# Layer 2's scores and values in narrow groups of the TensorE array, and its softmax sums taken by ScalarE

## The chip, the cores and the metric

The kernel runs on one core of a Trainium2 chip. The metric is the device time of one execution in microseconds, as the median of three runs. Everything is float32 except two small masks, and an f32 matmul leaves two records in the trace, each of them one pass over the columns of the moving operand.

## The reference

Four cross-attention layers run one after the other on `x` of shape (4, 1024, 256) with a context of shape (4, 77, 256); there are 16 heads. Layer 0 is causal self-attention together with the context, followed by a feed-forward block; layer 1 is a linear attention plus a windowed attention; layers 2 and 3 attend to the 77 context positions only. The change is in layer 2, whose heads are 16 wide:

```python
q = (queries @ Wq.T + bq)...; k = (keys @ Wk.T + bk)...; v = (values @ Wv.T + bv)...   # b h t 16
scores = einsum('bhqd,bhkd->bhqk', q, k) / sqrt(16)
scores = scores * attention_weights                      # (4, 16, 1024, 77), an input
scores = where(attention_mask, -inf, scores)             # an input too
out = einsum('bhqk,bhkd->bhqd', softmax(scores), v)...   # back to b t 256
x = queries + out @ Wo.T + bo                            # then a layer norm, then layer 3
```

## The kernel before

**Layers 0 and 1** take the first three quarters of the time. Each works through batches and quads of heads (`step`): bursts of matmuls for maxima or for weights and sums, and between the bursts pieces of other work, which `jobs0` and `jobs1` list as `Job` objects. A `Job` has a generator, a count of pieces, a stretch of the step in which the pieces are due, and for some a cost in microseconds by which pieces are fitted in. Layer 2's values and keys are made here, long before they are used: `values2` and `keys2` are jobs of batch 0, quad 0. Both write to DRAM (`kept_v`, `kept_k`) through the staging tile `stg` and others that `place` hands out in turn. All DMAs are issued by SyncE (SP) in program order; the next unit's `qk` tiles are filled by DMAs of the same queue (`new_unit`, L792, and `spread`, L377).

The values lie in `kept_v` on a block diagonal: for each half of the heads (8 of them, 616 rows of head and position) every row is 128 wide and holds its 16 values in its head's columns, with zeros elsewhere, which a first DMA writes from a zeroed `stg` (L970).

**Layers 2 and 3** run after that in one loop over slots, `slot23(i)`. There are 32 tiles of 128 queries (4 batches of 8). In slot `i` layer 2 does five stages, each of another tile:

- tile `i` (`a`): `score2` computes the scores of 16 heads x 77 positions = 1232 columns (`HK`), multiplies them with the input weights on VectorE (DVE; L1545), and puts a large negative number where the mask is set (L1550); `maxima2` takes each head's maximum (L1554, L1558);
- tile `i-1` (`p1`): `exps2` runs sixteen exponentials on ScalarE (ACT), one for each head with that head's maximum as bias (L1563); `sums_of` reduces them to the 16 sums on DVE (L1567) and takes the reciprocals (L1570); `divided` multiplies on GpSimd (POOL; L1574);
- tile `i-3` (`p3`): `turned_into` transposes the weights on TensorE (PE) in ten chunks of 128 columns, with three copies out of PSUM by ACT (`pT`, L1376);
- tile `i-4` (`p4`): `values_of2` multiplies the turned weights with `V`, 11 full-width matmuls (chunk 4 serves both halves of the heads) into `pvT`, and ACT copies the result to `oT` (L1593);
- tile `i-5` (`p5`): `out2` projects with `Wo`, `add2` adds to `x` (L1602 on DVE, L1603 on POOL).

Layer 3 follows 12 slots later (`LAG`) with stages of its own: `score3` (PE, then DVE L1626 and L1627), `exp3` (one exponential of 1232 columns, ACT L1643), `sums_of` and `divided`, `turned_into`, and `out3` (20 records into `po`, DVE L1639). So slots 0 to 11 hold layer 2 alone, slots 12 to 36 both layers, and the rest layer 3 alone. Between the stages `more()` runs pieces of side work: `prep2`, the next batch's query projections, and `between`, the norms between the layers. The engines work their queues in program order, and the order in `slot23` is written out by hand.

Score tiles (`pair_tile`) are two PSUM banks each, and there are two of them, shared by both layers. Smaller PSUM tiles (`psT`, `pvT`, projections) share a pool of three, and `po2` and `po3` share one bank. `score2` fills one score tile for each half of the heads, with two matmuls of 64 rows, each against a `kb` whose rows are zero outside the head in question (four heads, 308 columns):

```python
for o in range(2):
    ps = pair_tile()
    for e in range(2):
        r = half_rows(e)
        mm(ps[:, e, 0 : 4 * S].rearrange("p (h s) -> p h s", s=S),
           qT[r, o, P * t : P * t + P], kb[r, o, :, b, :])
```

`loads2(b)` loads a batch's `V` from `kept_v` with five DMAs, and clears part of it on POOL first (L1416); `load_sides` loads each tile's weights and mask.

Of the kernel before, what the change touches and what calls it, by code (L numbers as in the profile page):

```python
# [17 lines left out]
P = 128  # L18
# [13 lines left out]
def tile_xattn_seq(ctx: ExitStack, tc: tile.TileContext, d: dict, out: bass.AP):  # L32
# [899 lines left out]
    kept_g = dram.tile([P, 2, 8, 2, NS], F32, name="kept_g")  # L932
    kept_u = dram.tile([NB, H, S, D], F32, name="kept_u")

    HALF, DIAG = HH * S * P, S * P + DH
    kept_v = dram.tile([NB, 2, HH * DIAG], F32, name="kept_v")
    stg = wpool.tile([P, 1024], F32, name="stg", tag="s7")
    turn = [0]

# [25 lines left out]

    def values2():

        n = NB * 2 * HH * DIAG // P // 8
        nc.gpsimd.memset(stg[:, 0:n], 0.0)
        nc.sync.dma_start(  # L970
            out=kept_v.rearrange("b e x -> (b e x)").rearrange("(p k n) -> p k n", p=P, n=n),
            in_=stg[:, 0:n].unsqueeze(1).to_broadcast([P, 8, n]),
        )
        yield
        for b in range(NB):
            pk = sm.tile([S, D], F32, name="pk", tag="sm")
# [12 lines left out]
    def keys2():  # L989
# [419 lines left out]

    def loads2(b):  # L1410

        V = late.tile([P, NC + 1, P], F32, name="V2", tag="V2", bufs=2)
        lo, hi = [kept_v[b, e, 0:HALF].rearrange("(r n) -> r n", n=P) for e in range(2)]

        k = HH * S % P
        nc.gpsimd.memset(V[:, 4:6, :], 0.0)  # L1416
        nc.sync.dma_start(
            out=V[:, 0:4, :], in_=lo[0 : 4 * P].rearrange("(c p) n -> p c n", p=P)
        )
        nc.sync.dma_start(out=V[0:k, 4, :], in_=lo[4 * P :])  # L1420
        nc.sync.dma_start(out=V[k:P, 5, :], in_=hi[0 : P - k])
        nc.sync.dma_start(
            out=V[:, 6:10, :], in_=hi[P - k : 5 * P - k].rearrange("(c p) n -> p c n", p=P)
        )
        nc.sync.dma_start(out=V[0:HSIZE, 10, :], in_=hi[5 * P - k :])
        shared["v2", b] = V
        yield

# [97 lines left out]
    def score2(a, i):  # L1526

        b, t = a["b"], a["t"]
        qT, kb = shared["b2", b], shared["k2"]
        assert shared["ready2"] >= b  # L1530
        fs, mk = shared.pop(("side", i))
        if i + 1 < NB * NT:
            load_sides(i + 1)
        s = a["s"] = new_scores("s2", 4)
        for o in range(2):
            ps = pair_tile()
            for e in range(2):
# [6 lines left out]
            so = slice(o * HH * S, (o + 1) * HH * S)  # L1544
            nc.vector.tensor_tensor(  # L1545
                s[:, so].rearrange("p (i n) -> p i n", i=2), ps[:, :, 0 : 4 * S],
                fs[:, so].rearrange("p (i n) -> p i n", i=2), ALU.mult,
            )
        sv = s[:, 0:HK]
        nc.vector.copy_predicated(sv, mk, low.to_broadcast([P, HK]))  # L1550
# [7 lines left out]
        nc.vector.tensor_scalar(nm, nm, 0.1 * NEG, -SC, ALU.max, ALU.mult)  # L1558

    def exps2(a, heads):  # L1560
        for h in heads:
            hs = a["s"][:, S * h : S * h + S]
            nc.scalar.activation(hs, hs, AF.Exp, bias=a["nm"][:, h : h + 1], scale=SC)  # L1563

    def sums_of(a, tag):
        den = a["den"] = late.tile([P, H], F32, name=tag, tag=tag)
# [78 lines left out]
    def slot23(i, two, three, more):  # L1645
# [9 lines left out]
        if j < 0:  # L1655
# [13 lines left out]
                add2(p5)  # L1669
            more()  # L1670
            if p1:
                sums_of(p1, "den2")
                divided(p1)
            more()
        elif i < n + 5:
# [35 lines left out]
            more()  # L1711
            if p1:
                divided(p1)
# [36 lines left out]
    def jobs0(b, quad):  # L1750
# [7 lines left out]
        if b == 0 and quad == 0:  # L1758
# [205 lines left out]
```

## Time and profile before

| | |
|---|---|
| median of three runs | 2309.76 us (2304.88 to 2311.91) |
| profiled execution | 2310.56 us, span 2308.8 us, mean granted clock 0.982 |
| PE busy | 2158.3 us, 93% of the span |
| PEld (weight loads) | 1358.9 us, 59% |
| DVE busy | 1506.8 us, 65% |
| ACT busy | 1027.5 us, 45% |
| POOL busy | 652.2 us, 28% |
| DMA | 93.98 MB, mean 41 GB/s |

Busy shares are averages over stages that differ. Layers 2 and 3 take about the last 590 us; their first tile's mask lands at 1725 us, and layer 3's first scores stand at 1828 us. In a group's line the columns are line, engine, operation, names written and read, shape and count, then busy time, the mean of one in ns, and the engine's idle time before them with what ended it. Records of consecutive instructions overlap (a record runs until its own result is out), so for a run of matmuls the time from its first start to the next run's first start is what it takes.

### The profile page before, as it was taken

Reading aid. Unit: us, or ns where it says so; the run is one execution under the profiler, and the core shown is the slowest. Engines: PE = TensorE matmul, PEld = TensorE weight load, DVE = VectorE, ACT = ScalarE, POOL = GpSimd, SP = SyncE. Lnnn points to the kernel's source line nnn. Section 1 sums busy time; section 2 is a strip of 40 time slices with the busy share of each in tenths; the row PEclk is TensorE's granted clock in tenths of the full one; section 3 lists DMA queues with packets and bytes.
Section 4 is the critical chain, followed back from the end, with each engine's and each line's share of the span. In section 5 each row is a group of like instructions: output and inputs, shape, how many; then the busy total and the mean of one; then the engine's idle time right before and its main releaser. Section 6 shows DMA issues by size and latency. Waiting matters only on the chain.

```text
span 2308.8 us, 41140 instructions
## 1 busy us (share of the span) xinstructions
PE 2158.3 (93%) x16842; PEld 1358.9 (59%) x16874; DVE 1506.8 (65%) x2476; ACT 1027.5 (45%) x1716; POOL 652.2 (28%) x959
## 2 busy tenths in 40 slices
PE   4999999999999999999989999999988899999999
PEld 2544444555555455554556665666656678788877
DVE  3756567755566455754375666777748888788654
ACT  1144444434444444344533444544547655555322
POOL 2011113111131112310152233333333444444432
PEclk9899999999999999999989999999999999999999
DMA  7221121100000000101000010111025412313000
GB/s 217 55 57 68 31 65 41 40 6 15 7 15 2 10 11 6 38 1 19 6 15 6 15 26 16 21 20 20 15 74 152 136 51 68 100 49 95 10 10 17
DMA packets 87858, 93.98 MB, mean 41 GB/s; under 512 B 35714, under 2 KB 77558, under 8 KB 87542
## 3 DMA queue, kind: packets, MB, share of 16 engines
q1 hardware_dynamic: 87670, 91.35, 15.2%
q8 instruction: 133, 2.18, 0.4%
q14 instruction: 55, 0.45, 0.1%
HBM read 55.31 MB, written 18.39 MB: 32 GB/s over the span
## 4 chain that ended last, share of the span: by engine, by line
PE 67%; DVE 15%; ACT 4%; issue 2%; POOL 2%; DMA 0%; DVEq 0%; ACTq 0%; POOLq 0%; SPq 0%
PE ps L51 26%; PE po L51 12%; PE pv L51 6%; PE pp L51 5%; PE ph L51 4%; DVE mpart L672 3%; PE pvT L51 2%; DVE ms L1138 2%; PE ppv L51 2%; PE psT L1375 2%; PE pvw L51 1%; DVE mrow L1142 1%; PE pm L590 1%; PE pt L607 1%; ACT pe L738 1%
## 5 line engine op out<-in xcount | busy, mean ns | idle before, releaser
L51 PE MATMUL ps<-qk 32*128 32x192 f32 (+9 forms) x6528 | 581.8, 428 | 57.9 <-DVE mpart L672 25.1
L738 ACT ACTIVATE pe<-ps 128x1024 f32<-128x1024 f32 (+2 forms) x384 | 363.3, 952 | 589.5 <-PE ps L51 579.9
L51 PEld LDWEIGHTS ps<-qk 32*128 32x128 f32 (+1 forms) x6528 | 315.8, 185 | 295.6 <-issue 75.3
L672 DVE TENSOR_REDUCE mpart<-ps 128x2 f32<-128x1024 f32 (+4 forms) x384 | 331.0, 885 | 241.6 <-PE ps L51 240.8
L741 POOL TENSOR_SCALAR_AFFINE_SELECT pe<-pe 128x256 f32<-128x256 f32 (+1 forms) x192 | 95.2, 497 | 665.3 <-ACT pe L738 664.3
L1214 ACT ACTIVATE pew<-ps 128x768 f32<-128x768 f32 x128 | 103.4, 812 | 196.4 <-PE ps L51 196.4
L1574 POOL TENSOR_TENSOR s<-s,den 128x1232 f32<-128x1232 f32 x64 | 144.2, 2254 | 130.2 <-DVE den L1570 125.2
L1219 POOL TENSOR_SCALAR_AFFINE_SELECT pew<-pew 128x512 f32<-128x512 f32 x128 | 81.9, 640 | 337.7 <-ACT pew L1214 337.6
L1138 DVE TENSOR_TENSOR ms<-ps,maskw 128x768 f32<-128x768 f32 x128 | 122.1, 954 | 69.6 <-PE ps L51 68.1
L51 PE MATMUL po<-U,pT 128*128 128x256 f32 (+1 forms) x640 | 147.2, 385 | 10.8 <-DVE x L1602 7.6
L51 PE MATMUL pv<-pe,va 128*32 128x512 f32 (+3 forms) x1536 | 157.1, 496 | 0.0
L51 PE MATMUL ph<-yT,w 128*128 128x256 f32 x512 | 143.1, 401 | 2.4 <-DVE va L401 1.0
L51 PEld LDWEIGHTS po<-U,pT 128*128 128x128 f32 (+1 forms) x640 | 120.3, 192 | 35.0 <-ACT pT L1376 19.6
L51 PEld LDWEIGHTS po<-w,hT 128*128 128x128 f32 x800 | 111.8, 193 | 47.7 <-issue 38.9
L51 PE MATMUL ps<-G,xT 128*128 128x308 f32 x512 | 139.2, 422 | 0.0
L51 PE MATMUL po<-w,hT 128*128 128x128 f32 (+1 forms) x800 | 138.1, 317 | 0.9 <-ACT hT L904 0.9
L1563 ACT ACTIVATE s<-s,nm 128x77 f32<-128x77 f32 x512 | 134.8, 358 | 5.9 <-DVE nm L1558 5.9
L1376 ACT COPY pT<-psT 128x512 f32<-128x512 f32 (+1 forms) x192 | 87.7, 522 | 105.8 <-PE psT L1375 105.2
L665 DVE TENSOR_REDUCE mpart<-ps 128x8 f32<-128x1024 f32 x64 | 78.2, 1225 | 82.6 <-PE ps L51 80.0
L51 PEld LDWEIGHTS ph<-yT,w 128*128 128x128 f32 x512 | 88.8, 192 | 64.0 <-issue 50.8
L1142 DVE TENSOR_REDUCE mrow<-ms 128x4 f32<-128x768 f32 x128 | 122.2, 955 | 4.4
L51 PEld LDWEIGHTS ps<-G,xT 128*128 128x128 f32 x512 | 94.3, 190 | 30.1
(202 smaller groups left out, 3297.6 us busy)
## 6 DMA issues: line engine op xcount, KB each, us to landing
side<-in_fside_t SPq DMA_DIRECT2D x32, 616.0 KB
qk<-st SPq DMA_DIRECT2D x256, 64.0 KB
side<-in_mask_t SPq DMA_DIRECT2D x32, 154.0 KB
G<-kept_g SPq DMA_DIRECT2D x4, 1232.0 KB
U<-kept_u SPq DMA_DIRECT2D x4, 1152.0 KB
x<-in_x SPq DMA_DIRECT2D x8, 512.0 KB
out<-x SPq DMA_DIRECT2D x32, 128.0 KB
kept_g<-st SPq DMA_DIRECT2D x22, 154.0 KB
```

The costliest lines, as they stand in the source:

```text
L51: nc.tensor.matmul(o, lhsT, rhs, start=start, stop=stop, **kw)
L665: nc.vector.tensor_reduce(mpart[self.own][:, :, 2 * p : 2 * p + 2, 0].rearrange("p t j -> p j t"), ps.rearrange("p j (t n) -> p j t n", n= ...
L672: nc.vector.tensor_reduce(mpart[bl][:, i, 2 * p : 2 * p + 2, ci], ps[:, :, o : o + w], axis=AX.X, op=ALU.max,)
L738: nc.scalar.activation(pp[:n, :, o:512], ps[:n, :, o:512], AF.Exp, scale=SC)
L741: nc.gpsimd.affine_select(out=own, in_=own, compare_op=ALU.is_ge, fill=0.0, base=0, pattern=[[0, 2], [0, k], [1, P]], channel_multiplier=-1,)
L1138: nc.vector.tensor_tensor(v, ps.rearrange("p j (i n) -> p j i n", i=2)[:, :, :, 0:n], (maskw[:, 1:2] if w else maskw).unsqueeze(1).to_broa ...
L1142: nc.vector.tensor_reduce(mo, v, axis=AX.X, op=ALU.max, negate=True)
L1214: nc.scalar.activation(pp[:, :, :, 0 : P + WIN], ps.rearrange("p j (i n) -> p j i n", i=2)[:, :, :, 0 : P + WIN], AF.Exp, scale=SC,)
L1219: nc.gpsimd.affine_select(out=pf[:, :, 0:P], in_=pf[:, :, 0:P], compare_op=ALU.is_ge, fill=0.0, base=0, pattern=[[0, 4], [1, P]], channel_ ...
L1376: nc.scalar.copy(pT[:, 4 * group : 4 * group + n, :], ps[:, 0:n, :])
L1563: nc.scalar.activation(hs, hs, AF.Exp, bias=a["nm"][:, h : h + 1], scale=SC)
L1574: nc.gpsimd.tensor_tensor(s3, s3, a["den"].unsqueeze(2).to_broadcast([P, H, S]), ALU.mult)
```

## The change

- `values2` writes each head's values once into `kept_w`, 32 columns wide: a pair of heads (154 rows, `PAIR`) shares the 32 columns, each head in its own 16 and zeros in the other's.
- A new job, `spread2`, copies from `kept_w` to `kept_v` within DRAM. `CUTS` lists the 17 pieces into which the chunks of 128 and the pairs of 154 cut each other; each cut is a 128 x 32 block, zero outside its rows. There is one DMA for each cut, for all batches. `spread2` and `keys2` run in batch 0, quad 1.
- `loads2` is one DMA, without the clearing on POOL.
- `score2` uses 32 rows of the array for two heads at a time: eight matmuls of 154 columns, in four row groups that write four banks. Both score tiles are taken first, and a multiplication covers two banks (two groups, both halves).
- `values_of2` runs 17 matmuls of 32 columns; the four pairs of a half stand in four column groups, and the order goes round the groups.
- `exps2` gives each exponential an `accum_out`, which writes that head's sum into `den2`; DVE's reduction is gone from layer 2 and its reciprocal stays.
- In slots with both layers, `out2` and `add2` move ahead of the transposes of `p3`.

```diff
-    HALF, DIAG = HH * S * P, S * P + DH
-    kept_v = dram.tile([NB, 2, HH * DIAG], F32, name="kept_v")
+    PAIR = 2 * S
+    CUTS = [
+        (c, q, max(P * c, PAIR * q), min(P * c + P, PAIR * q + PAIR))
+        for q in range(HH) for c in range(PAIR * q // P, (PAIR * q + PAIR - 1) // P + 1)
+    ]
+    kept_w = dram.tile([NB, HK, HP], F32, name="kept_w")
+    kept_v = dram.tile([NB, P, len(CUTS), HP], F32, name="kept_v")
...
     def values2():
-        n = NB * 2 * HH * DIAG // P // 8
+        n = len(CUTS) * HP
         nc.gpsimd.memset(stg[:, 0:n], 0.0)
         nc.sync.dma_start(
-            out=kept_v.rearrange("b e x -> (b e x)").rearrange("(p k n) -> p k n", p=P, n=n),
-            in_=stg[:, 0:n].unsqueeze(1).to_broadcast([P, 8, n]),
+            out=kept_v.rearrange("b p k n -> p b (k n)"),
+            in_=stg[:, 0:n].unsqueeze(1).to_broadcast([P, NB, n]),
+        )
+        nc.sync.dma_start(
+            out=kept_w.rearrange("b (s q) n -> s b (q n)", s=S),
+            in_=stg[:S, 0 : H * HP].unsqueeze(1).to_broadcast([S, NB, H * HP]),
         )
...
             for e in range(2):
-                to = kept_v[b, e].rearrange("(j x) -> j x", x=DIAG)[:, 0 : S * P]
                 nc.sync.dma_start(
-                    out=to.rearrange("j (s p) -> s j p", p=P)[:, :, 0:DH],
-                    in_=v[:, P * e : P * e + P].rearrange("s (j r) -> s j r", r=DH),
+                    out=kept_w[b].rearrange("(q e s) n -> e s q n", e=2, s=S)[e, :, :, DH * e : DH * e + DH],
+                    in_=v.rearrange("s (q e r) -> s q e r", e=2, r=DH)[:, :, e, :],
                 )
+            yield
+
+    def spread2():
+
+        for k, (c, q, lo, hi) in enumerate(CUTS):
+            nc.sync.dma_start(
+                out=kept_v[:, lo - P * c : hi - P * c, k, :], in_=kept_w[:, lo:hi, :]
+            )
             yield
...
     def loads2(b):
-        V = late.tile([P, NC + 1, P], F32, name="V2", tag="V2", bufs=2)
...
+        V = late.tile([P, len(CUTS), HP], F32, name="V2", tag="V2", bufs=2)
+        nc.sync.dma_start(out=V, in_=kept_v[b])
...
         s = a["s"] = new_scores("s2", 4)
+        pair = [pair_tile() for _ in range(2)]
         for o in range(2):
-            ps = pair_tile()
-            for e in range(2):
-                r = half_rows(e)
+            for g in range(4):
+                e = 2 * (g % 2)
                 mm(
-                    ps[:, e, 0 : 4 * S].rearrange("p (h s) -> p h s", s=S),
-                    qT[r, o, P * t : P * t + P],
-                    kb[r, o, :, b, :],
+                    pair[g // 2][:, g % 2, PAIR * o : PAIR * o + PAIR].rearrange(
+                        "p (h s) -> p h s", s=S
+                    ),
+                    qT[rows_of(g), o, P * t : P * t + P], kb[rows_of(g), o, e : e + 2, b, :],
+                    skip_group_check=True,
                 )
...
+        for k in range(2):
             nc.vector.tensor_tensor(
...
+                of_pair(s, k),
+                pair[k][:, :, 0 : 2 * PAIR].rearrange("p i (o n) -> p i o n", o=2),
+                of_pair(fs, k), ALU.mult,
             )
...
     def exps2(a, heads):
+        if "den" not in a:
+            a["den"] = late.tile([P, H], F32, name="den2", tag="den2")
         for h in heads:
             hs = a["s"][:, S * h : S * h + S]
-            nc.scalar.activation(hs, hs, AF.Exp, bias=a["nm"][:, h : h + 1], scale=SC)
+            nc.scalar.activation(
+                hs, hs, AF.Exp, bias=a["nm"][:, h : h + 1], scale=SC,
+                accum_out=a["den"][:, h : h + 1],
+            )
...
-        for k in range(NC + 1):
-            o, c = (0, k) if k < 5 else (1, k - 1)
-            r = slice(0, rows_in(c))
-            mm(pv[:, o, :], V[r, k, :], a["pT"][r, c, :], start=k in (0, 5), stop=k in (4, NC))
+        for o in range(2):
+            own = [
+                [(k, c) for k, (c, q, _, _) in enumerate(CUTS) if q == 4 * o + j] for j in range(4)
+            ]
+            for n in range(max(map(len, own))):
+                for j in range(4):
+                    if n < len(own[j]):
+                        k, c = own[j][n]
+                        mm(
+                            pv[rows_of(j), o, :], V[:, k, :], a["pT"][:, c, :],
+                            start=(n == 0), stop=(n == len(own[j]) - 1), skip_group_check=True,
+                        )
...
             if p1:
-                sums_of(p1, "den2")
+                nc.vector.reciprocal(p1["den"], p1["den"])
                 divided(p1)
...
+            if p5:
+                out2(p5)
+                add2(p5)
             if p3:
                 turned_into(p3, "pT2")
             if c:
                 exp3(c)
             if p1:
-                sums_of(p1, "den2")
-            if p5:
-                out2(p5)
-                add2(p5)
+                nc.vector.reciprocal(p1["den"], p1["den"])
...
             j.append(Job(values2(), 5, 0.3, 0.9, us=0.85))
+        if (b, quad) == (0, 1):
+            j.append(Job(spread2(), len(CUTS), 0.1, 0.9))
             j.append(Job(keys2(), 4, 0.5, 0.9, us=0.5))
```

More of the change, by code (lines that the diff above doesn't have):

```diff
@@ L1410, in loads2 @@
     def loads2(b):
-        V = late.tile([P, NC + 1, P], F32, name="V2", tag="V2", bufs=2)
[L1413 to L1425, printed above, removed]
+        V = late.tile([P, len(CUTS), HP], F32, name="V2", tag="V2", bufs=2)
+        nc.sync.dma_start(out=V, in_=kept_v[b])
         shared["v2", b] = V
@@ L1534, in score2, with of_pair @@
         s = a["s"] = new_scores("s2", 4)
+        pair = [pair_tile() for _ in range(2)]
         for o in range(2):
-            ps = pair_tile()
-            for e in range(2):
-                r = half_rows(e)
-                mm(
-                    ps[:, e, 0 : 4 * S].rearrange("p (h s) -> p h s", s=S),
-                    qT[r, o, P * t : P * t + P],
-                    kb[r, o, :, b, :],
-                )
-            so = slice(o * HH * S, (o + 1) * HH * S)
+            for g in range(4):
+                e = 2 * (g % 2)
+                mm(
+                    pair[g // 2][:, g % 2, PAIR * o : PAIR * o + PAIR].rearrange(
[3 more added lines that the diff above has]
+                    skip_group_check=True,
+                )
+        def of_pair(v, k):
+            v = v[:, 0:HK].rearrange("p (o g n) -> p g o n", o=2, g=4)
+            return v[:, 2 * k : 2 * k + 2]
+        for k in range(2):
             nc.vector.tensor_tensor(
-                s[:, so].rearrange("p (i n) -> p i n", i=2), ps[:, :, 0 : 4 * S],
-                fs[:, so].rearrange("p (i n) -> p i n", i=2), ALU.mult,
+                of_pair(s, k),
+                pair[k][:, :, 0 : 2 * PAIR].rearrange("p i (o n) -> p i o n", o=2),
+                of_pair(fs, k), ALU.mult,
             )
```

## The prediction

> **What bounds the kernel now.** I read the stretches of layers 2 and 3 first (busy microseconds by engine: PE, PEld, DVE, ACT, POOL, then the granted clock and DMA), because all but a sliver of the change runs there.
>
> ```profile
> 1725.00:1833.00 108.00, 90.78 (x533) 69.22 (x530) 93.58 (x123) 73.76 (x247) 40.19 (x48) 0.91 0.40 120
> 1833.00:2000.00 167.00, 164.41 (x932) 131.62 (x931) 136.58 (x203) 94.08 (x263) 78.44 (x93) 1.00 0.32 95
> 2000.00:2170.00 170.00, 163.79 (x954) 136.83 (x953) 144.23 (x207) 88.65 (x255) 75.21 (x89) 0.99 0.19 57
> ```
>
> There are two regimes. From 1833 to 2170 layers 2 and 3 run together and TensorE is busy 328.20 of 337 us: PE time taken out of a slot comes off the end. From 1725 to 1833 layer 2 runs alone, and no engine is full. The chain of waits, asked for 1780 to 1797, says what paces a plain slot there:
>
> ```profile
> 1781.39 1.61 DVE s L1550
> ...
> 1783.02 1.45 DVE nm L1554
> ...
> 1784.58 0.42 DVE x L1602
> 1784.99 1.35 DVE den L1567
> ...
> 1786.55 1.45 DVE s L1545 x2
> 1787.99 0.02 issue
> 1788.02 1.63 DVE s L1550
> ```
>
> VectorE runs without a gap, 6.63 us a slot (1781.39 to 1788.02). The timeline gives ScalarE's exponentials in that slot and, further on, TensorE's scores and values:
>
> ```profile
> 1784.81 4.11 ACT L1563 ACTIVATE s<-s,nm 128x77 f32<-128x77 f32 x16
> ...
> 1892.00 2.62 PE L51 MATMUL pvT<-pT,V 128*128 128x128 f32 x22
> ...
> 1894.46 4.31 PE L51 MATMUL ps<-G,xT 128*128 128x308 f32 x16
> ...
> 1901.75 1.31 PE L51 MATMUL ps<-kb,qT 64*128 64x308 f32 x8
> ...
> 1902.99 3.29 PE L51 MATMUL po<-U,pT 128*128 128x256 f32 x14
> ```
>
> An f32 matmul leaves two records, each one pass over its columns. Start to next start, the values take 2.46 us (1892.00 to 1894.46) and the scores 1.24 us (1901.75 to 1902.99). What narrow groups side by side cost is shown by layer 0, which uses them already (32 rows by 128 columns for scores, 128 by 32 for values). The timeline of TensorE alone:
>
> ```profile
> 603.47 1.06 PE L51 MATMUL pv<-pe,va 128*32 128x512 f32 x8
> 604.46 1.16 PE L51 MATMUL po<-w,hT 128*128 128x128 f32 x8
> 605.55 0.71 PE L51 MATMUL ps<-qk 32*128 32x256 f32 x8
> 606.20 1.07 PE L51 MATMUL pv<-pe,va 128*32 128x384 f32 x16
> ...
> 611.20 0.64 PE L51 MATMUL pv<-pe,va 128*32 128x256 f32 x8
> 611.77 1.16 PE L51 MATMUL po<-w,hT 128*128 128x128 f32 x8
> ```
>
> Last, the groups by form from 1740 to the end, for the price of an exponential and of the sum:
>
> ```profile
> L1563 ACT ACTIVATE s<-s,nm 128x77 f32<-128x77 f32 x480 | 126.5, 359 | 4.9 <-DVE nm L1558 4.9
> L1567 DVE TENSOR_REDUCE den<-s 128x16 f32<-128x1232 f32 x63 | 89.6, 1422 | 4.1 <-ACT s L1643 3.9 <-issue 0.3
> L1643 ACT ACTIVATE s<-s 128x1232 f32<-128x1232 f32 x32 | 39.7, 1242 | 42.3 <-DVE s L1627 42.3
> ```
>
> **Values.** 11 full matmuls become 17 of 32 columns in five rounds of up to four (the second half's third round has one). Column-group rows: 8 records of 512 columns take 0.99 us, 8 of 256 take 0.57, so 0.205 ns per column and record, and 0.15 us fixed. Five full rounds are 40 x 128 = 5120 columns: 1.05 + 0.15 = 1.20; only the 34 records that exist: 4352 columns, 1.04. Entering a narrow mode from full width costs another 0.09 us by the start-to-start times of such pairs in the trace. I take 1.31 - the dearer count, because the lone cut stands last. Saving: 2.46 - 1.31 = 1.15 us a tile; between 1.33 and, if the groups ran only two by two, about 0.3.
>
> The Trainium skill (TensorEngine Tiling (Array Packing), section Theoretical Speedup) promises up to 4x for 32 columns; that would be 0.61 us, a saving of 1.85 a tile, and 24 tiles of it would put the time about 17 us under my forecast. The rows above are why I don't take it.
>
> **Scores.** Four matmuls of 64 rows and 308 columns become eight of 32 rows and 154 columns: 16 records, 2464 columns. The row-group burst of 8 x 256 = 2048 columns took 0.65 us (605.55 to 606.20); 416 more at 0.205 ns give 0.74. Saving 0.50 us a tile; modes were switched before too. Each multiply (L1545) now waits for both halves of the scores, so the first may start 0.1 us later; behind it on DVE stand the other multiply and the mask. With layer 3 beside it PE is what is full, alone DVE gains slack below, so I cost it at nothing. Both score buffers are taken at once; their last readers, layer 3's subtractions, end while PE runs about 2 us of transposes.
>
> **Sums.** The reduction L1567 goes for layer 2: 32 x 1.42 = 45 us of DVE work. With both layers it lies beside PE and is worth nothing; alone it is 1.35 us of a 6.63 us slot. The reciprocal stays and, as before, waits for the last exponential. In its place each of 512 exponentials also writes a sum. No row shows that. Below: nothing (a gain is excluded, the exponential itself stays). Above: a whole second short ACT instruction; from 359 ns at 77 columns and 1242 at 1232 the slope is 0.765 ns, the fixed part 0.30 us. Sixteen exponentials take 4.11 us, one every 0.256, so 0.10 us of each record overlaps the next. The nearest row is that overlap: if a sum must be out before the next starts, it is lost. I take e = 0.10 us each and keep 0 and 0.30.
>
> The Trainium skill speaks against me here: VectorE: DVE Perf Modes (section Two Vector instructions with no wait between them) counts an accumulator output as two instructions, on VectorE; if ScalarE did so at the fixed 280 ns less 93 ns overlap that ScalarE: Activation LUTs (What ACT_TABLE_LOAD costs) gives, an estimate of e is 0.19, and the sum below would come to about -20 us. The trace agrees with those figures for a plain exponential (359 ns, 0.10 overlap); no run here shows the read.
>
> **Layer 2 alone.** ScalarE's slot is sixteen exponentials, oT (0.37) and three pT copies (1.35), 5.9 us with small gaps; with e it is 5.9 + 16e, against VectorE's 6.63 - 1.4 = 5.2. The maxima (L1554) start at 1733.74, 1754.60 (three plain slots, 20.9 us), 1776.39 (two with the next batch's projections, 21.8), 1804.90 (four, 28.5) and 1828.24 (two with the norms' chain, 23.3). The seven plain slots go from 49.4 to 7 x 7.5 + 1.1 (two norms) = 53.6: +4. The two with projections lose some PE work: -2. The chain of norms I leave. Together +2 at e = 0.10; -9 at 0, where ScalarE's 5.9 rules; +18 at 0.20; +35 at 0.30. Here ScalarE takes VectorE's place as the bound.
>
> **Layers 2 and 3 together.** Values of tiles 8 to 31 and scores of tiles 12 to 31 fall in full PE slots: 24 x 1.15 + 20 x 0.50 = 37.6 us. DVE was 280.8 of 337 busy and sheds 1.4 a slot, ACT 182.7 and takes 1.6, so PE stays the bound with about the same room; I leave 3 us to small stalls as slots shorten: -35. Moving out2 and its add ahead of the transposes shortens waits that were small (PE for x L1602, 15 us in all from 1740 on, mostly inside other cover): nothing.
>
> **Layer 0.** keys2 moves one quad on, with eight DVE products (0.59 us each, 4.7 us) out of 70 to 100 (DVE 25.83 of 30) into 100 to 130 (14.78 of 30), and with its eight DMAs on SP. SP gets 17 DRAM-to-DRAM copies of 128-byte pieces, some 0.4 us to issue each as L999's rows, 7 us if all stood in the way; the first waits for the last kept_w write, and behind it are the next unit's qk transfers. Those ended at 148 us and are used near 157, and DMA was 6% busy from 100 to 130: hidden. The zero fill shrinks from 2.5 to 1.7 MB. Per batch, loads2 issues one DMA for five and drops POOL's memset (0.31 us), beside other work. Together -1, between -3 and +7.
>
> **The sum.** -35 + 2 - 1 = -34 us on a profiled execution of 2310.56 (span 2308.8 and 1.76 around it, 0.8 above the median of the three runs): 2276.6; against the median about 1 less. I say 2277.
>
> **Rivals.**
> - The sum costs no time (e = 0): -45, 2265. For it: the additions could ride in the pipe. Against: a second output per instruction.
> - The read is a larger part of an instruction (e = 0.20): -35 + 18 - 1 = -18, 2292.
> - PE's gain is half lost as waits: pT copies wait behind longer exponentials in ScalarE's queue (PEld waited 19.6 us on pT already). -17 + 2 - 1 = -16, 2294.
> - Slower: ScalarE becomes the bound everywhere, by the sums. At e = 0.30 layer 2 alone loses 35, and together ScalarE has 182.7 + 20 x 4.8 = 279 us of work in some 302; stalls then eat at least 10 of the 35. +35 - 25 - 1 = +9, 2319. It decides from e of about 0.27. Against it: it needs no overlap at all and a full second instruction.
>
> **Chances.** Forecast 0.50, e = 0: 0.10, e = 0.20: 0.20, half lost: 0.12, slower: 0.08. A measurement of this kernel tells about 0.3% (7 us) from no change. The first four lie below 2303 but for their edges: faster 0.88, same 0.04, slower 0.08. The range runs from 2260 (e = 0 and the cheaper count of the values) to 2300 (half lost, with e a little above 0.10); the slower case and such edges stay out.
>
> **What would show it.** Right: pvT from its first record to the next group near 1.25 us, scores near 0.74; exponentials alone every 0.36 us with ScalarE the chain of plain layer-2 slots at about 7.5 us; PE still over 95% busy with both layers. Wrong: exponentials 0.45 us apart or more; pvT at 2 us; PE idle for ACT pT over 30 us; a gap in layer 0 that ends on a qk transfer.

## The result: slower by about 1%, and the profile after

The changed kernel takes 2331.68 us (median of four runs, 2329.05 to 2334.93), the kernel before 2309.81 on the same chip; the ratio is 1.0095, with a 95% interval of 1.0075 to 1.0115. The profiled execution took 2334.93 us with a span of 2333.2, which is 24.4 more than the span of before. The prediction (2277, range to 2300) missed on the sign.

The span is best cut at three instructions which both kernels have: the first maxima of layer 2 (the start of the first L1554, now L1566), those of tile 12 (layer 3 has just joined) and those of tile 31 (the last).

| us | layers 0 and 1 | layer 2 alone | both layers | tail | span |
|---|---|---|---|---|---|
| before | 1728.4 | 99.8 | 315.9 | 164.7 | 2308.8 |
| after | 1752.7 | 109.0 | 309.5 | 162.0 | 2333.2 |
| difference | +24.3 | +9.1 | -6.4 | -2.7 | +24.4 |

So layers 0 and 1, of which layer 0 was costed at -1 and layer 1 at nothing, lose as much as the whole kernel; layer 2 alone loses 9 and not 2; and of the 35 us that both layers and the tail were to give, 9 came.

**The operations cost what was forecast.** TensorE's timeline of the kernel after, in a slot of layer 2 alone (start, us, operation):

```profile
1803.15 0.81 PE L51 MATMUL ps<-kb,qT 32*128 32x154 f32 x16
1803.89 1.13 PE L51 MATMUL po<-w2q,oT 128*128 128x256 f32 x4
1804.95 1.28 PE L51 MATMUL pvT<-pT,V 128*32 128x128 f32 x34
1806.16 1.09 PE L1391 MATMUL psT<-ident,s 128*128 128x128 f32 x8
```

Start to next start, the scores take 0.74 us (forecast 0.74, before 1.24), and the values 1.21 (forecast 1.31, before 2.46). The groups of the kernel after, from 1740 on by form (count, then busy time and mean ns of one), show how ScalarE adds up:

```profile
L1577 ACT ACTIVATE s<-s,nm 128x77 f32<-128x77 f32 x512 | 176.6, 360 | 3.7 <-DVE nm L1570 3.5
L1577 ACT ACTIVATION_READ_ACCUMULATOR s<-s,nm 128x1 f32 x512 | 103.0, 201 | 0.0
```

The exponential itself is as long as before (359 ns), and a second instruction reads the sum. Records overlap, so starts count: a plain exponential followed the one before after 0.249 us, now the next follows after 0.342. So e, the prediction's name for what one sum costs, is 0.093 us, against 0.10 in the prediction.

**Layer 0.** TensorE's timeline from 150 to 180 has one long gap (idle time and what ended it in brackets):

```profile
155.84 0.66 PE L590 MATMUL pm<-ident,mrow 128*128 128x128 f32 x4
173.93 2.37 PE L51 MATMUL ps<-qk 32*128 32x461 f32 x8 [17.43 <-DMA qk<-st]
```

Against before, the row maxima of the first four units of layer 0 start between 3.2 us early and on time; the fifth starts 19.3 late (202.0 against 182.7), and the later ones of layer 0 stay 19 to 21 late; where layers 0 and 1 lose the last 3 of their 24.3 us was not looked for. The waits of SP's queue from 60 to 215 say what the transfer stood behind (us in all, times, longest; first before, then after):

```profile
SPq L80 <- PE pk L51: 7.5, 1, 7.5
SPq L80 <- PE pk L51: 61.3, 1, 61.3
```

L80 is a load of layer 3's weight `wo`. It is issued at the start of quad 1 into the tile that holds layer 2's key and value weights, so it has to wait for the last matmul of `keys2`. In the kernel before that was soon over, and L80 went out at 94.79 us after a wait of 7.5. With the keys one quad later it went out at 148.52, and SP issues in program order: behind it came `spread2`'s 17 copies (0.55 to 1.2 us of issue each) mixed with the next unit's qk transfers. SP's timeline, two lines of before and four of after:

```profile
94.79 0.40 SPq L80 DMA_DIRECT2D l3wo<-in_L_wo  x1
112.92 35.23 SPq L377 DMA_DIRECT2D qk<-st  x8
...
148.52 0.40 SPq L80 DMA_DIRECT2D l3wo<-in_L_wo  x1
...
158.47 2.50 SPq L377 DMA_DIRECT2D qk<-st  x4
161.01 5.75 SPq L1000 DMA_DIRECT2D kept_v<-kept_w  x7
...
171.16 2.54 SPq L377 DMA_DIRECT2D qk<-st  x4
```

So the qk transfers went out at 158.47 to 160.96 and at 171.16 to 173.7, where before they had left by 148.1. While TensorE stood, the granted clock (the share of its full clock that TensorE was given) fell (columns as in the prediction's first fence):

```profile
160.00:180.00 20.00, 6.07 (x28) 2.10 (x28) 1.12 (x1) 1.13 (x2) 0.00 (x0) 0.50 0.52 114
```

**Layer 2 alone.** The stretch, then the chain of waits through a plain slot, both after:

```profile
1752.70:1861.70 109.00, 72.53 (x695) 50.14 (x694) 73.06 (x105) 87.00 (x426) 39.47 (x46) 0.85 0.38 116
```

```profile
1810.90 3.73 ACT s L1577 x22
1814.63 0.19 issue
1814.82 1.57 ACT s L1577 x9
1816.39 0.26 ACT oT L1618
1816.65 0.55 ACT pT L1392 x2
1817.20 0.29 issue
1817.49 0.39 ACT pT L1392
1817.88 3.73 ACT s L1577 x22
```

As forecast, ScalarE has taken VectorE's place as the chain, and a plain slot is 6.98 us (1810.90 to 1817.88; before 6.63 by VectorE). But the loss is not there. By the starts of the maxima, seven plain slots took 21.0 + 28.2 = 49.2 us, before 49.4; the two with the next batch's query projections 28.1, before 21.8; the two with the norms 26.1, before 23.3. The chain through the second projection slot shows why (`xT` is the transposed input, `pp` the projection, `qT` the projected queries):

```profile
1795.85 0.48 ACT xT L1444
...
1796.47 0.64 PE psT L1391 x4
...
1797.82 5.41 PE pp L51 x8
...
1803.26 0.02 ACT qT L1467
1803.28 0.56 issue
1803.85 3.81 ACT s L1577 x22
```

The same eight projections in the chain of the kernel before, first and second projection slot:

```profile
1756.72 5.27 PE pp L51 x8
1768.75 3.70 PE pp L51 x8
```

It is a loop of two engines. The copy of `xT` stands in ScalarE's queue behind the exponentials, the projections wait for that copy, and the next exponentials stand behind the projections' `qT` copy. So all 16 x 0.093 = 1.5 us go straight onto each of the two slots. In the second one TensorE, idle for 2.8 us ahead of its transposes, also does the projections at a lower clock, in 5.41 us at a granted clock of 0.68 where before it took 3.70 at 1.00; in the first they ran at the lower clock before too (0.65, now 0.67). That is 4.7 of the 6.3 us; the rest of it, and the 2.8 us of the slots with the norms, were not worked out.

**Both layers.** The stretch, before and after:

```profile
1828.20:2144.10 315.90, 309.80 (x1779) 252.46 (x1778) 268.48 (x393) 172.28 (x492) 145.44 (x174) 1.00 0.28 83
1861.60:2171.20 309.60, 293.08 (x2170) 227.48 (x2171) 240.62 (x374) 201.52 (x803) 144.93 (x174) 0.99 0.27 80
```

TensorE's wait for the copies `pT` in it, before, and its two longest waits after:

```profile
PE po L51 <- ACT pT L1376: 0.7, 3, 0.2
...
PE po L51 <- ACT pT L1392: 9.3, 16, 1.2
PE ps L51 <- DVE s L1652: 3.5, 4, 0.9
```

TensorE's busy time fell by 16.7 us (309.8 before), the stretch only by 6.4. Taking each run of matmuls from its start to the next run's start, 19 tiles of values went from 46.6 to 23.0 us, a little more than was promised. The scores went from 30.5 to 31.1: at 0.50 us a tile their matmuls save 9.5, but idle time behind them rose from 6.1 to 10.3, and the records spread. The transposes went from 43.0 to 49.3, and `out3`'s rounds from 79.2 to 84.5. A slot's boundary shows the wait (timeline after):

```profile
1899.98 1.35 ACT L1392 COPY pT<-psT 128x512 f32<-128x512 f32 x3 [3.95 <-PE psT L1391]
1901.20 1.26 ACT L1668 ACTIVATE s<-s 128x1232 f32<-128x1232 f32 x1
1901.92 0.81 PE L51 MATMUL ps<-kb,qT 32*128 32x154 f32 x16
1902.34 1.36 ACT L1392 COPY pT<-psT 128x512 f32<-128x512 f32 x3
1902.98 2.21 PE L51 MATMUL po<-U,pT 128*128 128x256 f32 x9 [0.26 <-ACT pT L1392]
```

`po<-U` (`out3`) needs layer 3's copies, which start at 1902.34. They stand in ScalarE's queue behind layer 3's exponential of the tile after (L1668, 1.26 us), and that behind layer 2's three copies. TensorE has two batches of ten transposes and the scores to fill that time; with narrow scores it runs out.

### The profile page after: what moved, and what is told of

Same layout as the page of the kernel before. It is cut to its first block, busy times and chain, and to the rows that moved or that the text cites. A ratio compares the mean times of both kernels' runs of the same rounds, so it can differ in the third digit from the quotient of the medians.

```text
span 2333.2 us, 42950 instructions
## 1 busy us (share of the span) xinstructions
PE 2140.0 (92%) x17514; PEld 1317.4 (56%) x17514; DVE 1461.8 (63%) x2444; ACT 1073.5 (46%) x2228; POOL 649.5 (28%) x955
## 3 DMA queue, kind: packets, MB, share of 16 engines
q1 hardware_dynamic: 87829, 89.79, 14.9%
## 4 chain that ended last, share of the span: by engine, by line
PE 64%; DVE 14%; ACT 7%; issue 2%; POOL 2%; DMA 0%; DVEq 0%; SPq 0%; ACTq 0%
PE ps L51 25%; PE po L51 12%; PE pv L51 6%; PE pp L51 6%; PE ph L51 4%; DVE mpart L672 3%; DVE ms L1154 2%; ACT s L1577 2%; PE ppv L51 2%; PE pvw L51 1%; DVE mrow L1158 1%; PE pt L607 1%; PE pm L590 1%; ACT pe L738 1%; ACT pT L1392 1%
## 5 line engine op out<-in xcount | busy, mean ns | idle before, releaser
L51 PE MATMUL ps<-qk 32*128 32x192 f32 (+9 forms) x6528 | 588.5, 429 | 73.2 <-DVE mpart L672 23.3
L1577 ACT ACTIVATE s<-s,nm 128x77 f32<-128x77 f32 x512 | 176.6, 360 | 3.7 <-DVE nm L1570 3.5
L1391 PE MATMUL psT<-ident,s 128*128 128x128 f32 x640 | 88.3, 279 | 31.9 <-ACT oT L1618 15.2
```

Of the source, the lines that this page charges most:

```text
L51: nc.tensor.matmul(o, lhsT, rhs, start=start, stop=stop, **kw)
L1391: nc.tensor.transpose(ps[:, k, :], s[:, P * c : P * c + P], ident)
```

## The experiments

The theories were: the late keys block SP's queue (layers 0 and 1); ScalarE's sums cost layer 2 alone its time; and a chain through ScalarE's queue at the slot boundary, made worse by the moved output rounds, eats the gain where both layers run. The main rival was that narrow groups or the sums cost the time themselves. All times are medians, ratios are against the kernel before on the same chip; stretches are those of the profiled execution. The first five rows add up, each with one change more.

| us | median | ratio (95%) | layers 0, 1 | 2 alone | both | tail |
|---|---|---|---|---|---|---|
| after | 2331.68 | 1.0095 (1.0075 to 1.0115) | 1752.7 | 109.0 | 309.5 | 162.0 |
| after, keys back | 2309.47 | 0.9995 (0.9983 to 1.0007) | 1728.1 | 107.0 | 310.5 | 163.1 |
| + output rounds back | 2301.82 | 0.9960 (0.9947 to 0.9973) | 1731.8 | 107.1 | 302.9 | 158.3 |
| + layer 3's exponential later | 2286.11 | 0.9891 (0.9870 to 0.9912) | 1728.0 | 108.9 | 293.7 | 154.4 |
| + choice by stage | 2273.72 | 0.9840 (0.9817 to 0.9864) | 1725.9 | 98.5 | 292.1 | 154.5 |
| before, sums by ScalarE | 2318.99 | 1.0044 (1.0027 to 1.0060) | 1729.1 | 105.7 | 317.0 | 164.4 |
| before, exponential later | 2308.23 | 0.9978 (0.9967 to 0.9989) | 1729.5 | 99.8 | 314.9 | 162.6 |
| before, keys late | 2316.28 | one run, no interval | 1734.3 | 98.2 | 317.3 | 164.7 |
| narrow groups alone | 2295.20 | 0.9930 (0.9906 to 0.9954) | 1732.1 | 101.2 | 302.4 | 158.6 |
| narrow values alone | 2291.87 | 0.9913 (0.9891 to 0.9935) | 1726.7 | 98.2 | 302.0 | 158.6 |
| narrow groups alone, exponential later | 2290.50 | 0.9913 (0.9892 to 0.9934) | 1731.4 | 101.2 | 300.8 | 158.2 |
| exponential later, wide scores | 2290.14 | 0.9900 (0.9884 to 0.9915) | 1729.4 | 107.5 | 296.7 | 154.5 |

The columns tell more than the medians. With the keys back, layers 0 and 1 are the same code in all variants of the changed kernel, and they took 1725.9 to 1732.1 us; so a difference of a few us between two medians can come from a stretch that the edit does not touch.

**Keys back in quad 0, in the changed kernel.**

```diff
 (b, quad) == (0, 0):
+            j.append(Job(keys2(), 4, 0.5, 0.9, us=0.5))
 (b, quad) == (0, 1):
             j.append(Job(spread2(), len(CUTS), 0.1, 0.9))
-            j.append(Job(keys2(), 4, 0.5, 0.9, us=0.5))
```

> The changed kernel with keys2 back in batch 0, quad 0, spread2 left in quad 1. Theory A: the 20.7 us that layer 0 lost before its fifth maxima come from the load of layer 3's wo, which reuses the tile that keys2 reads: it stands in SP's queue ahead of the next unit's qk transfers and waited 61 us for keys2. Then this run comes out 19 to 24 us below the changed kernel, at 2308 to 2313, and layer 2's first scores start near 1725 us again. Rival B: the 17 copies of spread2 fill SP's queue and the DMA rings: then most of the loss stays, 2325 or more. Layers 2 and 3 take as long as in the changed kernel by both.

The median fell by 22.2 us, the stretch of layers 0 and 1 by 24.6. The line of SP's waits, in this run:

```profile
SPq L80 <- PE pk L51: 6.0, 1, 6.0
```

One job's place cost 22 us, and `spread2`'s 17 copies alone, still in quad 1, cost nothing: every one of the first nine row maxima of layer 0 starts within 0.2 us of before.

**Only the keys late, in the kernel before** (the same job moved to quad 1, nothing else changed).

> The kernel before with keys2 moved to quad 1 and nothing else. Theory A: the loss appears whole, 2329 to 2334, in one gap in front of the fifth maxima of layer 0, with SP waiting some 60 us ahead of the load of wo. Rival B: within 3 us of the kernel before, since there is no spread2.

The time of its one run was 2316.28, some 5 us above the kernel before and not the 20 or so that the theory asked for, although the wait was all there:

```profile
SPq L80 <- PE pk L51: 61.1, 1, 61.1
```

From the fourth maxima to the fifth it took 5.7 us longer than before (33.7 against 28.0), in the changed kernel 20.7 longer: the qk transfers left right behind the load, at 151.64 to 155.0 and 156.23 to 158.6. So the theory was half right. The late keys shut the queue for 61 us, and that alone costs some 6. What makes it 20.7 is that the copies, costless by themselves, stand among the qk transfers when the queue opens: the last four of these went out 14.9 us later than here (171.16), and the issue of the fifteen copies ahead of them takes 12.2 us of that. Another 3.3 us there is a wait of SP for ScalarE (L792), which is 0.4 us at most in this run.

**Output rounds behind layer 3's exponential again** (with the keys back).

```diff
-            if p5:
-                out2(p5)
-                add2(p5)
             if p3:
                 turned_into(p3, "pT2")
             if c:
                 exp3(c)
             if p1:
                 nc.vector.reciprocal(p1["den"], p1["den"])
+            if p5:
+                out2(p5)
+                add2(p5)
```

> As e1, with out2 and add2 back behind layer 2's transposes and exp3. Theory C: with the projection moved away from between them, twenty transposes of two tiles stand in a row and wait for ScalarE's copies out of three PSUM buffers, which is the 6 us that the transposes gained in 19 slots: 5 to 8 us below e1, transposes back near 116 ns a record. Rival: the waits belong to the chain of layer 3's subtraction, exp3 and pT copies, which ends at the same time wherever the projection stands: within 3 us of e1.

7.7 us faster by the medians, as large as expected, so the move that was costed at nothing cost at least that. By the stretches it is 7.6 in both layers and 4.8 in the tail, against 3.7 more in layers 0 and 1, which the move does not touch. It did not come where I expected it: the transposes kept their pace (137 ns a record, 133 with the move), and the scores with the wait behind them fell from 31.1 to 25.1. Layer 2's output rounds stand between the transposes again and give the copies time. The wait became smaller and did not go:

```profile
PE po L51 <- ACT pT L1392: 6.5, 8, 1.0
```

**ScalarE's sums alone, in the kernel before** (`accum_out` on the 512 exponentials, the reduction on VectorE left out).

> The kernel before with the sums taken by the exponentials, nothing else. By the read of 0.093 us each seen in the changed kernel: layer 2 alone about 0.3 us longer in each of seven plain slots (+2 us); with both layers TensorE is the bound and DVE is relieved of work that was covered: nothing. 2308 to 2314. Rival D: ScalarE's 1.5 us more in each full slot delays the pT copies that TensorE waits for, about 1 us in each of 20 slots: 2325 or more.

7.5 us slower than the kernel before on that chip (2311.50; by the ratio it is 10), of which 5.9 lie in layer 2 alone (105.7 against 99.8): 3.0 in the two projection slots, 3.3 in the two with the norms, and nothing in the plain ones. That is more than I expected, and not where; where both layers run the sums change little (+1.1), and TensorE's wait for the copies `pT` is 0.7 us as before.

**Sums back on VectorE** (keys and output rounds back; only the narrow groups are left of the change).

> The changed kernel with the keys in the first quad, the output rounds of layer 2 behind layer 3's exponential as before, and the sums of the weights on VectorE (23 per tile) in place of ScalarE's accumulating form: of the change only the narrow values and scores are left. Theory of the sums (the accumulating form costs ScalarE 16 x 0.093 us per tile; where layer 2 stands alone ScalarE is the chain, and TensorE, waiting longer, runs at half clock for longer): layer 2 alone, which took 99.8 us before and 107.1 with the accumulating form, goes to 97 to 101 us, both layers stay at 302 to 306 us, the whole is 2291 to 2297 us (2301.8 with the accumulating form). Rival (what layer 2 alone lost comes from the narrow values and scores, not from the sums): layer 2 alone stays above 104 us and the whole at 2299 to 2304 us.

2295.20 us, ratio 0.9930 (0.9906 to 0.9954); layer 2 alone 101.2, both layers 302.4. The sums' theory holds: 5.9 us come back in layer 2 alone, next to none elsewhere. (The 23 instructions of the expectation are wrong: VectorE's sums are one reduction and one reciprocal a tile.) The projections of the second projection slot, 5.41 us in the chain above, are in this run's chain

```profile
1772.64 3.70 PE pp L51 x8
```

**Wide scores as well** (the same kernel with the old `score2`; narrow values alone are left).

> As the kernel with the narrow groups alone (keys in the first quad, output rounds as before, sums on VectorE), with the score rounds of layer 2 in the old four wide rounds: of the change only the narrow values are left. Theory of the chain (the 0.5 us per tile that the narrow scores save is paid back as waiting, since the scores stand right ahead of a wait for the copies of layer 3's weights): both layers within 3 us of the kernel with narrow scores, and the whole within 4 us of it. Rival (TensorE's time counts wherever it is saved): 0.5 us x 31 tiles = 15 us more, of which 9 or 10 where both layers run.

2291.87 us, ratio 0.9913 (0.9891 to 0.9935): 3 us faster than with narrow scores, by intervals that overlap. Both layers take 302.0 (302.4 with narrow scores), so the 9.5 us that the narrow scores take off TensorE are all paid back as waiting, as the theory had it. Layer 2 alone takes 98.2 in place of 101.2. 1.1 us of that lie in the seven plain slots (49.3 and 50.4): with VectorE as the chain there, the narrow scores cost something, since in the chain of waits their two multiplications, which now read and write in strips, take 0.75 to 0.81 us each, and the old ones 0.72. Another 1.5 lie in the first projection slot, where the projections took 3.80 us in place of 5.01; that is not shown to come from the scores, for the kernel before and its variant with late keys, which have the same layer 2, differ there by 1.2.

**Layer 3's exponential later** (ScalarE's sums, keys and output rounds back).

```diff
             if c2:
                 turned_into(c2, "pT3")
+            if c1:
+                exp3(c1)
             if p1:
                 exps2(p1, range(4))
...
-            if c:
+            if c and i == n + 4:
                 exp3(c)
```

> The changed kernel with the keys in the first quad and the output rounds of layer 2 behind layer 3's exponential as before (2301.8 us), and one move more: where both layers run, the exponential of layer 3's tile is issued at the start of the next slot, behind that slot's copies of the layer 3 weights out of PSUM, not ahead of them. Theory of the chain (at the boundary of two slots TensorE waits for these copies, which stand in ScalarE's queue behind an exponential that waits for VectorE, which waits for the last score rounds): the wait goes, both layers take 286 to 297 us in place of 302.9, the whole 2287 to 2296 us. Rival (the chain is not what bounds the slot; TensorE or ScalarE is full): within 3 us of 2301.8. A second rival: the exponential then delays layer 2's exponentials in the same slot, and both layers take 305 to 312 us.

15.7 us faster by the medians; by the stretches 9.2 in both layers and 3.9 in the tail (layers 0 and 1 took 3.8 less and layer 2 alone 1.8 more, which the move does not touch). TensorE's waits where both layers run, the stretch itself, and a slot's boundary:

```profile
PE psT L1391 <- DVE xT L1446: 5.2, 4, 1.3
PE ps L51 <- DVE s L1652: 0.9, 4, 0.2
PE po L51 <- ACT pT L1392: 0.5, 2, 0.3
```

```profile
1837.00:2130.60 293.60, 286.94 (x2172) 224.99 (x2172) 243.10 (x373) 201.87 (x803) 144.42 (x174) 1.00 0.29 84
```

```profile
1875.43 1.35 ACT L1392 COPY pT<-psT 128x512 f32<-128x512 f32 x3 [0.61 <-PE psT L1391]
1875.92 0.81 PE L51 MATMUL ps<-kb,qT 32*128 32x154 f32 x16
1876.65 1.25 ACT L1668 ACTIVATE s<-s 128x1232 f32<-128x1232 f32 x1
1876.65 2.64 PE L51 MATMUL po<-U,pT 128*128 128x256 f32 x11
```

The copies now start when their transposes are done and the exponential follows them; `po<-U` starts straight behind the scores. The wait for `pT` went from 9.3 us in the kernel after to 0.5, and TensorE is busy 98% of the stretch again. The wait that the expectation named was right; its inner part was not, mostly: in the boundary shown, the exponential was held up not by VectorE but by layer 2's copies ahead of it in the same queue (in all, ScalarE idled 8.9 us in front of it for VectorE, in five of the slots of the kernel after).

**The same move in the kernel before.**

> The kernel before with one move: where both layers run, layer 3's exponential is issued at the start of the next slot, behind that slot's copies of layer 3's weights. Theory (the chain by way of this exponential bounds the slot only once TensorE has been made shorter; in the kernel before TensorE is full, with 6 us of idle time behind the scores in 19 slots): both layers gain at most 6 us, the whole is 2303 to 2311 us. Rival (the chain bounded the kernel before too, so the gain of the move is not owed to the narrow groups): 8 to 16 us faster, 2294 to 2302 us.

4.0 us faster, 3.1 of it in both layers and the tail. The same three lines are worth 13.1 us there on the shortened kernel (15.7 by the medians): this chain was nearly hidden before. TensorE's wait for `pT` tells what uncovered it: 0.7 us in the kernel before, 0.7 with ScalarE's sums alone, 3.5 with the narrow groups and VectorE's sums, 6.5 with the narrow groups and ScalarE's sums (output rounds back). So the shorter TensorE work uncovers it, and the longer work of ScalarE adds to it.

**The same move with VectorE's sums.**

> The narrow groups alone (keys in the first quad, output rounds as before, sums on VectorE) and layer 3's exponential behind the next slot's copies of layer 3's weights. If the sums and the chain are two separate losses, the two gains add: layer 2 alone 97 to 101 us, both layers 286 to 297 us, the whole 2278 to 2290 us. Rival (VectorE's 23 instructions of sums per tile delay layer 3's scores and with them the chain, so that where both layers run the sums on VectorE cost what they save where layer 2 stands alone): the whole within 3 us of the kernel with the accumulating form and the same move.

2290.50 us, ratio 0.9913 (0.9892 to 0.9934). The gains do not add. Layer 2 alone is at 101.2, but both layers at 300.8: with the reductions (1.42 us a tile) back in VectorE's queue, the later exponential gains 1.7 us there and not 9. TensorE's wait for `pT` is as short as with ScalarE's sums (0.7 us), but another is now the longest:

```profile
PE po L51 <- DVE x L1622: 11.2, 11, 1.6
```

L1622 is VectorE's addition of layer 2's output, which stands in its queue behind that reduction, and `out3` gets the shared bank only behind it. With the exponential in its old place this wait was 8.6 us, with ScalarE's sums and the later exponential there is none. So ScalarE's sums do bring time where both layers run, but only once the exponential is out of the way: VectorE's 1.4 us was not free there, only hidden.

**Wide scores with the exponential later and ScalarE's sums.**

> The kernel with ScalarE's sums, the keys in the first quad, the output rounds as before and layer 3's exponential later (2286.1 us), with the score rounds of layer 2 in the old four wide rounds. Theory (with the chain out of the way TensorE is the bound where both layers run, so the 0.50 us per tile of the narrow scores count there, as they did not while the chain was in the way): both layers 302 to 305 us in place of 293.7, layer 2 alone 107 to 109 us as before, the whole 2294 to 2298 us. Rival (the narrow scores bring nothing): both layers within 3 us, the whole 2283 to 2289 us.

2290.14 us, ratio 0.9900 (0.9884 to 0.9915): the narrow scores are worth 4.0 us now, both layers 296.7 against 293.7. That lies between the theory (9 or more) and the rival (none). The scores' runs take 24.5 in place of 17.6 us, but the transposes give 2.7 back (49.9 to 47.2), since the wait of TensorE for VectorE's `xT` falls from 5.2 to 2.5. The 1 us or so that is left was not settled.

**A choice by stage.** Narrow values throughout; where layer 2 stands alone, wide scores and VectorE's sums; where both layers run, narrow scores and ScalarE's sums; keys and output rounds as before, the exponential later.

```diff
-    def score2(a, i):
+    def score2(a, i, alone):
...
-    def exps2(a, heads):
-        if "den" not in a:
+    def exps2(a, heads, add=True):
+        if add and "den" not in a:
...
-                accum_out=a["den"][:, h : h + 1],
+                **(dict(accum_out=a["den"][:, h : h + 1]) if add else {}),
```

> The same kernel with a choice by stage: where layer 2 stands alone, wide scores and sums on VectorE as before; where both layers run, narrow scores and ScalarE's sums; narrow values throughout. If the losses and gains of the stages are separate, layer 2 alone takes 97 to 101 us (98.2 with wide scores and VectorE's sums, 108.9 with the changed ones), both layers stay at 292 to 296 us, and the whole is 2273 to 2280 us. Rival (layer 2 alone is held back by something else than the scores and the sums): 2283 to 2289 us.

2273.72 us, ratio 0.9840 (0.9817 to 0.9864): 2.5% less than the changed kernel and 1.6% less than the kernel before. Layer 2 alone takes 98.5 us and both layers 292.1, so the stages add as expected.

## Why the prediction was wrong

- **Operations: right.** Values 1.21 us (1.31 said, where the prediction's own terms, 1.20 and 0.09, give 1.29), scores 0.74 (0.74), e = 0.093 (0.10). The Trainium skill (VectorE: DVE Perf Modes, Two Vector instructions with no wait between them) says of VectorE that an accumulator output is a second instruction. This trace shows ScalarE doing the same. The 0.19 us that I estimated was twice the measured cost: the read's record is 0.20 us long and not the 0.28 that I put in, while its overlap, 0.11, is near the 0.09 that I took off. The "up to 4x" of TensorEngine Tiling (Array Packing), section Theoretical Speedup, stayed out of reach as argued: 2.46 to 1.21 us is 2.0x.
- **Layer 0, said -1 (to +7), was +24: the step that failed.** I costed the eight products and eight DMAs of `keys2` and asked whether the qk transfers behind the copies were hidden. I did not ask who waits for `keys2`. The load of `wo` takes over its weight tile, and it stands in the one DMA queue ahead of all these transfers. "Hidden" was read off the slack at 148 us in a trace where that load had gone at 94.79. The last of the signs that I gave for being wrong, a gap in layer 0 that ends on a qk transfer, is what the trace shows. With the keys back in their place the stretch is 0.3 us shorter than before (2.5 shorter to 3.7 longer over all variants), so the rest of the term stood.
- **Layer 2 alone, said +2, was +9.** Direction and new bound (ScalarE) were right; two terms had their size wrong, in opposite ways. Plain slots, said +4, were -0.2: ScalarE's own work came to 6.98 and not 7.5 us, as overlapping records had been added up. Projection slots, said -2, were +6.3: I took them for TensorE's, but they are a loop of exponentials, `xT` copy and projections in series, where each read counts and in one of the two the clock is lower too. The norms, left out, were +2.8. The prediction is not of one mind here: its forecast counts the read in the seven plain slots alone, while its rivals price each further 0.10 us at 16 or 17 us, which is ten slots. By the runs the sums alone account for 5.9 of the 9.
- **Both layers and the tail, said -35, were -9.** The 37.6 us of TensorE time were real by the length of the unhindered runs (1.24 us a tile for the values, 0.50 for the scores). The 3 us set aside for stalls should have been 28.5. The rival "half lost" named the place (`pT` copies behind longer work in ScalarE's queue), but the work right ahead of them was layer 3's exponential and not layer 2's. With the output rounds back and the exponential later, both layers and the tail stand at -32.5 against before (293.7 + 154.4 against 315.9 + 164.7), of which the later exponential by itself is worth 3.1 (314.9 + 162.6 in the kernel before with that move). "Moving out2: nothing" was the second failed term here, 7.7 us by the medians and 12.4 by the two stretches.
- **The slower rival** had the sign and not the mechanism: it needed e above 0.27.

The term for -35 was thus about right for a kernel whose queues let TensorE run, and that kernel was not the one at hand. The 2273.7 us of the last version are near the 2277 of the sum, but that version has two changes which the prediction did not think of, so this does not speak for it.

## What to carry to other kernels

When a step is moved, list who waits for its last reader, not only what it issues: a load that takes over a tile holds every transfer behind it in its queue. When the bound engine is made shorter, follow one slot's boundary through the queues of the other engines: a copy behind an exponential, hidden before, became the wait when 1.7 us of matmuls went and 1.5 us of ScalarE's work came. And judge a trade between engines stage by stage: here the same sums by ScalarE cost 6 to 8 us in one stage and gain 7 in another.

## What the runs showed of the hardware

- ScalarE's accumulating form is two instructions: the read is a record of 0.20 us of its own and costs 0.093 us, start to start.
- Two costs in one queue can come to more than their sum. From the fourth to the fifth maxima of layer 0, 17 small copies cost 0 us (changed kernel), a load held for 61 us cost 5.7 us (kernel before), and both cost 20.7 us.
- VectorE's multiplications of the narrow scores, which go over the same 616 columns in strips, took 0.75 to 0.81 us where the contiguous ones took 0.72. That the strips are the cause was not tried by itself.
- In the layer 0 gap the granted clock was 0.50 from 160 to 180 us, so the matmuls that started at 173.93 ran at half speed for some 6 us: eight records of 461 columns took 2.37 us there, and 1.23 us at 202.12. The Trainium skill (TensorE: Matmul & The Clock Gate, What's actually happening) describes a gate that falls to half after an idle window of about 3.4 us and opens after a busy one, with windows that run on their own; these 6 us are within two such windows, so row and rule agree.
- `po<-U`, unchanged itself, took 4.52 us in the usual slot, 4.39 to 4.42 before, and 4.49 to 4.52 with wide scores and narrow values. It goes with the narrow values that follow it, and layer 0 of the kernel before has the like: the four records of `pm` take 0.53 us or more, start to next start, ahead of a narrow group and 0.44 or more ahead of a full-width one. That a change of the array's mode is what costs these 0.1 us is only argued.
